# Three map steps and three convolution rounds to a tick, and spectral matmuls placed by tile shape, in a two-layer convolution kernel

## The chip, the cores and the metric

The kernel runs on one core of one Trainium2 chip. The metric is device microseconds of one launch. All arithmetic is float32. TensorE is called PE in the profile, its weight loads PEld, VectorE DVE, ScalarE ACT, GpSimd POOL and SyncE SP.

## The reference, cut to what matters

The input is `x`, 8 batch elements of 8 channels of 512 x 512. Two layers follow each other, each with a group normalization `_gn` (4 groups of two channels) in front and a residual around it:

```python
x = x + L0(_gn(x))      # spectral layer
x = x + L1(_gn(x))      # coupled map, hidden convolution, gates
```

L0 takes every second row and column, goes to the spectrum (`rfft2`), keeps 8 x 4 low modes, mixes the channels there with complex weights, and synthesizes the result back on all 512 x 512 points:

```python
out2 = einsum('bixy,ioxy->boxy', FW1[low modes], w)      # mode by mode
tmp  = einsum('boxw,xz->bozw', out2, E1)                 # over the rows
x2   = real(einsum('bozw,wi->bozi', tmp, E2)) / (Ws*Hs)  # over the columns
```

L1 has three parts: 15 steps of a coupled map, a hidden convolution (3x3 to 128 channels, ReLU, 1x1 back to 8, sigmoid), and a gate that blends both:

```python
for _ in range(15):
    mapped = 3.9 * grid * (1 - grid)
    physics = 0.7 * mapped + 0.3 * conv3x3_per_channel(mapped)
    grid = 0.85 * physics + 0.15 * drive
h   = relu(conv3x3(x, Wp, bp));  nca = sigmoid(conv1x1(h, Wu, bu))
g   = sigmoid(conv1x1(relu(conv3x3(concat(x, cml, nca), Wg1)), Wg2))
out = g * cml + (1 - g) * nca
```

## The kernel before, in words

The program is one straight list of instructions, recorded by Python loops; `keep_order` pins the order on every engine to that of the source. So the loops below decide what stands behind what on each engine's queue.

**Map steps.** `Slabs` holds one of 4 sets per half of the channels: 16 slabs of 32 rows each, with halos, as one tile `m`. A last set `Tail` closes the bottom rows. An element has 9 sets and each takes 15 steps, so 135 steps. `convolve` (L524) is 48 matmuls of 32x32 tiles into a half of PSUM, `settle` drains it (VectorE L537, ScalarE L543), adds to the drive on POOL at steps 1 and 13 (L516, L547), and `renew` exchanges the halo rows by four DMAs from POOL's queue (L570, L571). The list `slots` orders the steps: step 1 of every set of a phase, then step 2 of every set, and so on. The first phase of an element has 4 sets, the second 5. So a set comes back 4 or 5 slots later, and by then its halo must have landed. At step 15 a set leaves (`leave`, L596).

**Rounds.** `Hidden.round` (L723) is one of 128 rounds of the hidden convolution of an element: 12 matmuls of 32x128 tiles into a PSUM half; ScalarE (L729) drains one pair of banks to `h`, VectorE (L731) the other. `Hidden.point` (L742) is the 1x1 convolution of finished rounds in 128x32 tiles; four rounds are summed in `y`, on which ScalarE then runs the sigmoid (L755).

**Gates.** `Gate` covers 12 image rows, 43 to an element, one element behind the map: loads of `gin` and `mix`, `conv` (L793, 128x32 tiles; POOL L798, VectorE L799 and L803), `point` (L810; sigmoid L814, POOL L816) and `finish` (VectorE L821, store L828).

**Spectral work.** `layer0` is a generator for the element after the present one. Every `yield` ends a piece and says when the next may run. The pieces are: statistics and row transform of a channel (L329, L333: 128x128 tiles), averages over partitions (`group_stats`, L300 and L308: 128x128), the column transform (L358), the mode mix on VectorE, `over_rows` of a channel (L396: 16x32) and `synthesis` of half a channel (L428: two products of 8x128, then one add L431 and two statistics L433 on VectorE).

**The tick.** `work` records one tick: two map steps (`near` and `far` half of PSUM), `others.finish()`, loads (`transfers`), up to two rounds, and then, in the banks left, a gate's convolution, spectral pieces, the points, and the gate product of an earlier tick's gate. The outer loop runs 68 ticks per element and spreads 128 rounds over them:

```python
ticks = (second.end - at + 1) // 2
quota = [(t + 1) * (rounds - done) // ticks for t in range(ticks)]
```

The last element has 56 rounds beside its steps; its other 72 rounds and all its 43 gates run after the last step. Ahead of element 0's first steps stand its own spectral layer and 8 rounds. `Slots` hands out 20 tile buffers of 8 KB per partition between the sets and the others (`SHARED`, `MORE` and `LEAST` bound the share of the others), and `AHEAD` is how many slots ahead of a phase its loads (`dE`, `dO`) may begin.

Of the kernel before, what the change touches and what calls it, by code (L numbers as in the profile page):

```python
# [41 lines left out]
P = 128  # L42
# [12 lines left out]
LONG, LATER, NEXT = -1, -2, -3  # L55
GATES_FROM, SPECTRAL_FROM = 1, 2
# [9 lines left out]
SLOTS, SHARED, MORE, LEAST = 20, 5, 8, 3  # L66
AHEAD, PAUSE = 12, 6
# [50 lines left out]
def conv_layers(ctx: ExitStack, tc: tile.TileContext, a, out):  # L118
# [79 lines left out]
    avg = cp.tile([P, P], F32, name="avg")  # L198
# [14 lines left out]
    e1 = cp.tile([16, N], F32, name="e1")  # L213
    e2 = cp.tile([P, N], F32, name="e2")
    om = cp.tile([16, C + 3, 8], F32, name="om")
# [6 lines left out]
    def sines():  # L222
# [14 lines left out]
        nc.scalar.dma_start(out=e1[8:], in_=t)  # L237
# [58 lines left out]
    def group_stats(mv, n, bank):  # L296

        mean = sm.tile([P, n], F32, name=f"mean{n}")
        ps = bank[-1][:, 0]
        nc.tensor.matmul(ps[:, :n], avg, mv[:, :, 0], start=True, stop=True)  # L300
        nc.vector.tensor_copy(mean, ps[:, :n])
        var = sm.tile([P, n], F32, name=f"var{n}")
        nc.vector.tensor_tensor(var, mv[:, :, 0], mean, ALU.subtract)
        nc.vector.tensor_tensor(var, var, var, ALU.mult)
        nc.vector.tensor_tensor(var, var, mv[:, :, 1], ALU.add)
        yield LATER
        ps = bank[-1][:, 0]
        nc.tensor.matmul(ps[:, :n], avg, var, start=True, stop=True)  # L308
        std = sm.tile([P, n], F32, name=f"std{n}")
        nc.scalar.activation(std, ps[:, :n], AF.Sqrt, bias=eps)  # L310
        rstd = sm.tile([P, n], F32, name=f"rstd{n}")
        nc.vector.reciprocal(rstd, std)
        return mean, rstd, std

    def layer0(e, bank):


        def one():
            return bank[-1][:, 0]

        st = sm.tile([P, C, 4, 6], F32, name="st")
        mys = sm.tile([P, C, 2, 32], F32, name="mys")


        for c in range(C):
            yield c
# [3 lines left out]
            my = one()[:, :64].rearrange("p (h k) -> p h k", h=2)  # L330
            for h in range(2):
                for j in range(2):
                    nc.tensor.matmul(  # L333
                        my[:, h], xt[:, 2 * j, h * NS : (h + 1) * NS : 2], dft_y[:, j],
                        start=(j == 0), stop=(j == 1),
                    )
# [3 lines left out]
        yield NEXT  # L340
# [10 lines left out]
        wmix, ts = row([16, 2, C, C, 4], "wmix"), row([16, 2, C, C, 4], "ts")  # L351
        nc.sync.dma_start(out=wmix, in_=a["wmix"])
        yield LATER
        mx = one()[:, : C * 8].rearrange("p (c k) -> p c k", k=8)
# [8 lines left out]
        nc.vector.tensor_copy(f, mx[:16].rearrange("p c (q k) -> p c q k", q=2))  # L363

# [12 lines left out]
        yield LATER  # L377
        re = total(0, 0, 1, 1, ALU.subtract, "re")
        yield LATER
# [4 lines left out]
        back = sm.tile([16, C, 4], F32, name="back_re")  # L384
        nc.vector.tensor_scalar(back, re, on_sin, -1.0, ALU.mult, ALU.mult)
        nc.vector.tensor_scalar(re, re, on_cos, None, ALU.mult)
        nc.vector.scalar_tensor_tensor(om[:, :C, 0:4], im, on_sin, re, ALU.mult, ALU.add)
        nc.vector.scalar_tensor_tensor(om[:, :C, 4:8], im, on_cos, back, ALU.mult, ALU.add)
        yield LATER
# [3 lines left out]
        def over_rows(c):  # L393
            ps = one()
            for at in range(0, P, 32):
                nc.tensor.matmul(  # L396
                    ps[at : at + 32], om[:, c : c + 4].rearrange("p c k -> p (c k)"), e1, start=True, stop=True, tile_position=(0, at)
# [39 lines left out]
        for c in range(C):  # L437
            yield C + c
            ty, xt = ty_next, e.x[C + c]
            if c % 2 == 0:  # L440
                st = sm.tile([P, 2, 4, 6], F32, name="st1", bufs=2)
            synthesis(ty, xt, st[:, c % 2], 0)
            if closing:
                yield LATER
                next(closing)
                yield LATER
                next(closing, None)
                closing = None
            if c + 1 < C:
                yield  # L450
                ty_next = over_rows(c + 1)
            yield LONG
            synthesis(ty, xt, st[:, c % 2], 1)
            if c % 2:
                closing = close(c // 2, aggregate(st, 1))
        for kind in (NEXT, LATER):
            yield kind
            next(closing, None)
# [11 lines left out]
    class Slabs:  # L470
# [122 lines left out]
        def leave(self):  # L593
# [4 lines left out]
            def store():  # L598
# [6 lines left out]
                later(1, lambda: sets.drop(m))  # L605
# [50 lines left out]
    class Phase:  # L656
# [12 lines left out]
        def ready(self, k, o, n):  # L669

            s = self.sets[k]
            due = self.at + k <= n + 1
# [7 lines left out]
        def squares(self, n):  # L680
            while self.squared < len(self.sets) and sets.room():
                if not self.ready(self.squared, 0, n + 2):
# [12 lines left out]
    class Hidden:  # L695
# [19 lines left out]
        def round(self, ps, after, settled):  # L715
# [12 lines left out]
            h = wk.tile([P, 4, N], F32, tag="h", name="h", bufs=2)  # L728
# [9 lines left out]
        def point(self, ps):  # L738

            for r, h in self.hs:  # L740
                for g in range(4):
                    nc.tensor.matmul(  # L742
                        ps[32 * g : 32 * g + 32], w_u[:, r % 4], h[:, g],
                        start=(r == self.hs[0][0]), stop=(r == self.hs[-1][0]),
                        tile_position=(0, 32 * g),
                    )
            if self.hs[0][0] % 4 == 0:
                self.y = wk.tile([P, N], F32, tag="y", name="y", bufs=1)
# [3 lines left out]
            self.hs.clear()  # L752
# [84 lines left out]
    class Element:  # L837


        def __init__(self, b):  # L840
# [15 lines left out]
            self.bank = []  # L856
            self.pieces, self.need = layer0(self, self.bank), None

        def fetch(self):

            if self.fetched < 2 * C and shared.room() > 0 and len(self.x) < self.most():
# [4 lines left out]
        def most(self):  # L866
            return 2 if self.fetched < C else 4 if self.fetched < 2 * C else 0
# [9 lines left out]
        def spectral(self, ps, n, longs):  # L877

            need = self.need
            if need == NEXT and now[0] <= self.last:  # L880
                return False
            if not self.pieces or need == LATER and n or need is not None and need >= LONG and longs:
                return False
            if need is not None and need >= 0 and now[0] <= self.at.get(need, now[0]):
                return False
            self.bank.append(ps)
            self.need, self.last = next(self.pieces, self), now[0]
            self.bank.clear()
            if self.need is self:
                self.pieces, self.need = None, None  # L890
            return True

    class Others:


        def __init__(self):
            self.before, self.after, self.limit, self.lag = None, None, 2, 0
            self.mapped, self.paused, self.closed = deque(), False, False
            self.loaded, self.convolved, self.pointed = deque(), deque(), deque()
            self.longs = 0  # L900

        def feed(self, t):
# [3 lines left out]
            spectral = after and after.pieces  # L906
            spectral = spectral and (t >= SPECTRAL_FROM or not e)
            kept = max(0, after.most() - len(after.x)) if spectral else 0
            while e and e.gates and t >= GATES_FROM and not (self.paused or self.closed):
                if len(self.loaded) == self.limit or shared.room() - kept < 2:  # L910
# [6 lines left out]
            if spectral:  # L917
                after.fetch()
# [8 lines left out]
        def point(self, ps):  # L927
            if not (self.convolved and self.convolved[0].at < now[0]):
                return False
            g = self.convolved.popleft()  # L930
            g.point(ps)
            self.pointed.append(g)
            return True

        def spectral(self, banks):
            if not self.after:
                return
            for n, ps in enumerate(banks):
                long = self.after.need is not None and self.after.need >= LONG
                if not self.after.spectral(ps, n, self.longs):  # L940
                    return
                self.longs += long

        def gate(self, ps):
            self.longs = 0
            if not (self.loaded and self.loaded[0].at + self.lag < now[0]):
                return False
            g = self.loaded.popleft()
            g.conv(ps)
# [219 lines left out]
```

## Time and profile before

| | before |
|---|---|
| median of 3 runs | 9446.41 us |
| lowest and highest | 9430.03 and 9450.78 us |
| the profiled execution, its own time | 9442.09 us |
| its span | 9440.3 us |
| mean granted TensorE clock | 0.986 |
| busy PE, DVE, ACT, POOL | 9039.4, 5657.6, 4072.3, 3367.1 us |
| DMA | 1327.07 MB, mean 141 GB/s |

The span is what the hardware profiler saw from the first to the last instruction. A float32 product is two records in it, so the 48 matmuls of a step are 96. A matmul's end is modelled, so the distance from the start of one group to the start of the next tells more than the length of a group. In a list of groups, "idle" is the time in which the engine did nothing just before them, and behind it stands what ended most of it; "issue" means that the profile shows nothing that was waited for.

### The profile page before, as it was taken

The numbers are of one execution on the slowest core, as the hardware profiler recorded it, in microseconds if no ns is written. First come the engines' busy times: TensorE is split into PE (matmuls) and PEld (weight loads), VectorE is DVE, ScalarE is ACT, GpSimd is POOL, SyncE is SP. The second block draws the span as 40 slices with busy tenths as digits, with TensorE's granted clock in tenths as the row PEclk, the third lists the DMA queues.
The fourth block names the chain that finished last, engine by engine and source line by source line (L and its number), as shares of the span: only waits on it lengthen the run. The fifth ranks groups of instructions, "written<-read, shape, count | busy, mean of one in ns | idle before, by whom it ended". The sixth has DMA issues, their size and how long they took to land. (4 is left out here: it accounts for less than half of the span.)

```text
span 9440.3 us, 331607 instructions
## 1 busy us (share of the span) xinstructions
PE 9039.4 (96%) x148976; PEld 4068.9 (43%) x148976; DVE 5657.6 (60%) x5820; ACT 4072.3 (43%) x4285; POOL 3367.1 (36%) x4440
## 2 busy tenths in 40 slices
PE   6999999999999999999999999999999999999989
PEld 2444444444444444444444444444444444434433
DVE  5665566655666556665566555665566655555655
ACT  2444444444444444444444444444444444434422
POOL 3232333334333343433434333343433434343422
PEclk9999999999999999999999999999999999999999
DMA  4241365565645656655566556565565665565488
GB/s 148 87 128 35 90 168 136 146 142 136 164 129 150 143 127 160 157 138 139 145 149 165 137 125 156 129 169 139 127 169 136 165 138 117 141 155 124 109 198 207
DMA packets 697405, 1327.07 MB, mean 141 GB/s; under 512 B 146938, under 2 KB 152442, under 8 KB 668498
## 3 DMA queue, kind: packets, MB, share of 16 engines
q1 hardware_dynamic: 591840, 1244.38, 52.1%
q0 software_dynamic: 101792, 60.33, 3.1%
q8 instruction: 1171, 19.19, 0.9%
q14 instruction: 248, 2.03, 0.1%
q10 hardware_dynamic: 2354, 1.14, 0.0%
HBM read 977.48 MB, written 270.61 MB: 132 GB/s over the span
## 5 line engine op out<-in xcount | busy, mean ns | idle before, releaser
L524 PE MATMUL pair<-m,band 32*32 32x512 f32 x103680 | 3703.2, 604 | 159.3 <-issue 103.3
L543 ACT ACTIVATE m<-m 128x1024 f32<-128x1024 f32 x2016 | 2125.7, 1055 | 2458.2 <-DVE m L537 2396.4
L723 PE MATMUL pair<-cols,w_p 32*128 32x511 f32 (+1 forms) x24576 | 2863.4, 604 | 73.7 <-DMA cols<-xn 29.4
L524 PEld LDWEIGHTS pair<-m,band 32*32 32x32 f32 x103680 | 1997.7, 103 | 1788.1 <-issue 997.9
L570 POOL DMA_DIRECT2D m<-m x1568 | 861.4, 549 | 3927.7 <-ACT m L543 3851.5
L537 DVE SCALAR_TENSOR_TENSOR m<-pair,dO 128x1024 f32<-128x1024 f32 x1152 | 1357.0, 1220 | 1172.7 <-PE pair L524 1021.8
L723 PEld LDWEIGHTS pair<-cols,w_p 32*128 32x128 f32 x24576 | 1307.6, 187 | 1647.1 <-issue 1148.9
L731 DVE TENSOR_SCALAR h<-pair,b_p 128x1024 f32<-128x1024 f32 x1024 | 1312.8, 1283 | 905.5 <-PE pair L723 898.8
L537 DVE SCALAR_TENSOR_TENSOR m<-pair,dE 128x1024 f32<-128x1024 f32 x1008 | 1187.7, 1220 | 1064.3 <-PE pair L524 911.2
L729 ACT ACTIVATE h<-pair,b_p 128x1024 f32<-128x1024 f32 x1024 | 1140.0, 1114 | 923.3 <-PE pair L723 923.0
L742 PE MATMUL pair<-h,w_u 128*32 128x512 f32 x8192 | 1051.8, 606 | 39.3 <-ACT h L729 35.0
L793 PE MATMUL pair<-gin,w_g 128*32 128x511 f32 (+1 forms) x8256 | 962.2, 598 | 11.3 <-DMA gin<-nca 7.9
L816 POOL TENSOR_TENSOR mix<-mix 96x512 f32<-96x512 f32 x344 | 437.7, 1272 | 1278.7 <-ACT mix L814 1236.4
L571 POOL DMA_DIRECT2D m<-m x1568 | 841.3, 537 | 30.3 <-issue 27.2
L742 PEld LDWEIGHTS pair<-h,w_u 128*32 128x32 f32 x8192 | 244.7, 110 | 690.9 <-issue 347.8
L755 ACT ACTIVATE y<-y,b_u 128x512 f32<-128x512 f32 x256 | 184.8, 722 | 823.3 <-DVE y L751 823.3
L793 PEld LDWEIGHTS pair<-gin,w_g 128*32 128x32 f32 x8256 | 235.3, 110 | 686.8 <-issue 462.9
L798 POOL TENSOR_TENSOR mix<-mix 96x512 f32<-96x512 f32 x344 | 444.2, 1291 | 14.2 <-DMA mix<-nca 9.8
L547 POOL TENSOR_SCALAR dO<-dO 128x2048 f32<-128x2048 f32 x72 | 391.7, 5440 | 115.0 <-DVE m L537 114.0
L749 ACT COPY y<-pair 128x512 f32<-128x512 f32 x256 | 149.8, 585 | 624.2 <-PE pair L742 486.5
L516 POOL TENSOR_SCALAR dO<-dO,base 128x512 f32<-128x512 f32 x288 | 208.8, 735 | 574.6 <-DMA dO<-xn 532.7
L821 DVE SCALAR_TENSOR_TENSOR mix<-mix,back 96x512 f32<-96x512 f32 x344 | 329.1, 957 | 138.5 <-POOL mix L816 138.5
(90 smaller groups left out, 3337.1 us busy)
## 6 DMA issues: line engine op xcount, KB each, us to landing
gin<-xn SPq DMA_DIRECT2D x344, 384.0 KB
cols<-xn SPq DMA_DIRECT2D x256, 512.0 KB
x<-in_x SPq DMA_DIRECT2D x120, 1024.0 KB
gin<-cml SPq DMA_DIRECT2D x344, 320.0 KB
gin<-nca SPq DMA_DIRECT2D x344, 320.0 KB
dE<-xn SPq DMA_DIRECT2D x288, 256.0 KB
dO<-xn SPq DMA_DIRECT2D x288, 256.0 KB
mix<-xn SPq DMA_DIRECT2D x344, 192.0 KB
```

Source lines behind the costliest of these rows:

```text
L524: nc.tensor.matmul(ps[h // 2][32 * t : 32 * t + 32, h % 2], band[at, self.channel(step - 1, h, t), dx], m[at, t, dx : dx + N], start=(n == ...
L537: nc.vector.scalar_tensor_tensor(u[:, at], ps[q], FLOOR, d[:, at], ALU.max, ALU.add)
L543: nc.scalar.square(u[:, at], u[:, at])
L570: nc.gpsimd.dma_start(out=view(tb, rb, dims), in_=view(ta, ra, dims))
L571: nc.gpsimd.dma_start(out=view(ta, ra + s, dims), in_=view(tb, rb + s, dims))
L723: nc.tensor.matmul(ps[g // 2][:, g % 2, lo:hi], w_p[p, dx, i % 2], self.cols[p, i // 2, at : at + hi - lo], start=(n == 0), stop=(n == 2), ...
L729: nc.scalar.activation(h[:, :2], ps[0], AF.Relu, bias=b_p)
L731: nc.vector.tensor_scalar(h[:, 2:], ps[1], b_p, 0.0, ALU.add, ALU.max)
L742: nc.tensor.matmul(ps[32 * g : 32 * g + 32], w_u[:, r % 4], h[:, g], start=(r == self.hs[0][0]), stop=(r == self.hs[-1][0]), tile_position ...
L793: nc.tensor.matmul(ps[32 * j : 32 * j + 32, lo:hi], gband[:, dx], gin[:, j, at : at + hi - lo], start=(n == 0), stop=(n == 2), tile_positi ...
L798: nc.gpsimd.tensor_tensor(d, d, ng, ALU.subtract)
L816: nc.gpsimd.tensor_tensor(d, d, mix[: GR * C, 2], ALU.mult)
```

## The change

A tick has three map steps and up to three rounds instead of two and two. PSUM halves alternate from one use to the next (`half()`). Behind the rounds stand the pieces of kind `WIDE`: both halves of a channel's synthesis in one tick, in the other PSUM half. If one was placed, the 128x32 work of that tick uses the half of the last round. That work is: an `EARLY` spectral piece, a gate's convolution, the points (in one or two groups, as rounds of two sums can meet in a tick), a second gate or one or two `LATE` pieces, and the gate products of the same tick's gates; then gate loads. The row transform, the averages and `over_rows` become 128x32 tiles: four column tiles for the first two, and for the last `e1` and `om` are padded with zeros to 128 rows. `h` has three buffers and `y` two, the slots are 19, and up to two channels of `x` are loaded in a tick. After the last step every tick takes three rounds and up to two gates, of which the first waits three ticks.

```diff
-LONG, LATER, NEXT = -1, -2, -3
-GATES_FROM, SPECTRAL_FROM = 1, 2
+TICK = 3
+WIDE, EARLY, LATE = "wide", "early", "late"
+GATES_FROM, SPECTRAL_FROM = 1, 0
 SHIFTS = ((1, 0, N, 0), (0, 1, N, 0), (2, 0, N - 1, 1))
@@ -63,8 +64,8 @@
 TAIL_RENEW = 7
 TAIL_ROWS = ((1, SLAB - STEPS + TAIL_RENEW - 1), (STEPS - TAIL_RENEW + 1, SLAB))
 assert TAIL_AT + TAIL_ROWS[0][1] == N - SLAB + TAIL_ROWS[1][0]
-SLOTS, SHARED, MORE, LEAST = 20, 5, 8, 3
-AHEAD, PAUSE = 12, 6
+SLOTS, SHARED, MORE, LEAST = 19, 4, 7, 3
+AHEAD = 12
...
+    e1 = cp.tile([P, N], F32, name="e1")
+    nc.gpsimd.memset(e1, 0.0)
...
+        def averaged(v):
+            ps = bank[-1]
+            for at in range(0, P, 32):
+                nc.tensor.matmul(
+                    ps[at : at + 32, :n], avg, v, start=True, stop=True, tile_position=(0, at)
+                )
+            return ps[:, :n]
...
-            yield c
+            yield (LATE if c % 2 else EARLY), c
             xt = e.x[c]
             for j in range(4):
                 nc.vector.bn_stats(st[:, c, j], xt[:, j])
-            my = one()[:, :64].rearrange("p (h k) -> p h k", h=2)
+            my = bank[-1][:, :64].rearrange("p (h k) -> p h k", h=2)
             for h in range(2):
                 for j in range(2):
-                    nc.tensor.matmul(
-                        my[:, h], xt[:, 2 * j, h * NS : (h + 1) * NS : 2], dft_y[:, j],
-                        start=(j == 0), stop=(j == 1),
-                    )
+                    for q in range(4):
+                        at = h * NS + 64 * q
+                        nc.tensor.matmul(
+                            my[32 * q : 32 * q + 32, h], xt[:, 2 * j, at : at + 64 : 2],
+                            dft_y[:, j], start=(j == 0), stop=(j == 1),
+                            tile_position=(0, 32 * q),
+                        )
             nc.scalar.copy(mys[:, c], my)
             e.done_with(c)
...
-            yield C + c
-            ty, xt = ty_next, e.x[C + c]
+            yield WIDE, C + c
+            ty, xt, e.back_begun = ty_next, e.x[C + c], True
             if c % 2 == 0:
                 st = sm.tile([P, 2, 4, 6], F32, name="st1", bufs=2)
             synthesis(ty, xt, st[:, c % 2], 0)
+            yield WIDE, None
+            synthesis(ty, xt, st[:, c % 2], 1)
             if closing:
-                yield LATER
+                yield EARLY, None
                 next(closing)
-                yield LATER
+            if c + 1 < C:
+                yield LATE, None
+                ty_next = over_rows(c + 1)
+            if closing:
+                yield LATE, None
                 next(closing, None)
                 closing = None
-            if c + 1 < C:
-                yield
-                ty_next = over_rows(c + 1)
-            yield LONG
-            synthesis(ty, xt, st[:, c % 2], 1)
             if c % 2:
                 closing = close(c // 2, aggregate(st, 1))
-        for kind in (NEXT, LATER):
-            yield kind
+        for kind in (EARLY, LATE):
...
-            due = self.at + k <= n + 1
+            due = self.at + k < n + TICK
...
-            h = wk.tile([P, 4, N], F32, tag="h", name="h", bufs=2)
+            h = wk.tile([P, 4, N], F32, tag="h", name="h", bufs=TICK)
...
+        def sums(self):
+            groups = {}
             for r, h in self.hs:
+                groups.setdefault(r // 4, []).append((r, h))
+            self.hs.clear()
+            return list(groups.values())
+        def point(self, hs, ps):
+            for r, h in hs:
                 for g in range(4):
                     nc.tensor.matmul(
                         ps[32 * g : 32 * g + 32], w_u[:, r % 4], h[:, g],
-                        start=(r == self.hs[0][0]), stop=(r == self.hs[-1][0]),
+                        start=(r == hs[0][0]), stop=(r == hs[-1][0]),
                         tile_position=(0, 32 * g),
                     )
-            if self.hs[0][0] % 4 == 0:
-                self.y = wk.tile([P, N], F32, tag="y", name="y", bufs=1)
+            if hs[0][0] % 4 == 0:
+                self.y = wk.tile([P, N], F32, tag="y", name="y", bufs=2)
...
+            for _ in range(2):
+                if self.fetched == 2 * C or shared.room() == 0 or len(self.x) == self.most():
+                    break
                 self.x[self.fetched] = load_x(shared, self.b, self.fetched % C)
                 self.at[self.fetched] = now[0]
                 self.fetched += 1
-            return 2 if self.fetched < C else 4 if self.fetched < 2 * C else 0
+            if self.fetched == 2 * C:
+                return len(self.x)
+            return 4 if self.fetched < C or self.back_begun else 2
...
+        def conv(self, banks):
+            for n, ps in enumerate(banks):
+                if not self.loaded or now[0] < self.hold or self.loaded[0].at + self.lag > now[0]:
+                    return n
+                g = self.loaded.popleft()
+                g.conv(ps)
+                self.convolved.append((g, ps))
+            return len(banks)
+        def point(self):
+            while self.convolved:
+                g, ps = self.convolved.popleft()
+                g.point(ps)
+                self.pointed.append(g)
...
-    def work(steps, rounds, e, after, transfers, squares=lambda: None):
+    halves = pairs[:2], pairs[2:]
+    used = [0]
+    def work(steps, rounds, e, after, gates, transfers, squares=lambda: None):
+        def half():
+            used[0] += 1
+            return halves[used[0] % 2]
         settled = iter(())
-        near, far = pairs[:2], pairs[2:]
-        for (s, step), ps in zip(steps, (near, far)):
+        for n, (s, step) in enumerate(steps):
+            ps = half()
             s.convolve(step, ps)
             next(settled, None)
             settled = s.settle(step, ps)
             next(settled)
             others.finish()
+            if gates == 2:
+                others.load(1)
+                gates = 1
         others.finish()
         transfers()
-        for ps in (near, far)[:rounds]:
-            e.hidden.round(ps, after, settled)
+        for _ in range(rounds):
+            e.hidden.round(half(), after, settled)
         next(settled, None)
         squares()
-        if rounds == 2:
-            pairs.reverse()
-        elif rounds:
-            near, far = far, near
-        point = rounds and e.hidden.n % 2 == 0
-        gate = others.gate(near[0][:, 0])
-        others.spectral((far[0], far[1]) if gate else (near[0], far[0] if point else near[1]))
-        if point:
-            e.hidden.point(near[1][:, 0])
-        last = others.point((near[0] if point else near[1])[:, 1])
-        if not last:
-            others.spectral([near[0] if gate or point else near[1]])
-        if rounds == 0 and gate or rounds == 1 and not (gate or point or last or after):
-            pairs.reverse()
+        if not others.spectral(WIDE, halves[(used[0] + 1) % 2]):
+            used[0] += 1
+        b = [ps[:, i] for ps in halves[used[0] % 2] for i in range(2)]
+        others.spectral(EARLY, b[3:])
+        others.conv(b[:1])
+        groups = e.hidden.sums()
+        for hs, ps in zip(groups, b[1:3]):
+            e.hidden.point(hs, ps)
+        if not others.conv(b[3:]):
+            others.spectral(LATE, [b[1] if len(groups) == 2 else b[2], b[3]])
+        others.point()
+        others.load(gates)
...
-        steps = [slots[i] for i in (at, at + 1) if 0 <= i < len(slots)]
-        work(steps, rounds, e, after and after.hidden, transfers, squares)
-    for at in range(-FIRST_ROUNDS, 0, 2):
-        turn(at, 2, e, None, -1)
+        steps = [slots[i] for i in range(at, at + TICK) if 0 <= i < len(slots)]
+        work(steps, rounds, e, after and after.hidden, gates, transfers, squares)
...
+        open_ = [
+            t >= GATES_FROM and at + TICK * t < second.end - AHEAD
+            and not first.end - AHEAD + 3 <= at + TICK * t < first.end + 3
+            for t in range(ticks)
+        ]
...
+            left = len(others.before.gates) if others.before else 0
+            gates = open_[t] + (left > sum(open_[t:]) and not (after and after.pieces))
+            turn(at, min(more, TICK), e, after, gates)
+            at += TICK
...
+    others.after, others.hold, others.lag = None, now[0] + 3, 2
+    sets.most = shared.most = SLOTS
+    while e.hidden.n < ROUNDS or others.mapped or others.busy():
+        turn(at, min(TICK, ROUNDS - e.hidden.n), e, None, 2 if len(others.loaded) <= 4 else 0)
+        at += TICK
```

## The prediction

> **What bounds the kernel now.** I read the page's engine rows first, then TensorE's stretches in order of time, then TensorE's waits.
>
> ```profile
> PE 9039.4 (96%) x148976; PEld 4068.9 (43%) x148976; DVE 5657.6 (60%) x5820; ACT 4072.3 (43%) x4285; POOL 3367.1 (36%) x4440
> ```
>
> TensorE is busy 96% of the span, the next engine 60%. So the time is the sum of TensorE's stretches plus what stops it. In the view of one engine in order of time (start, length, engine, line, operation, tiles, tile shape, count), one whole tick of before is:
>
> ```profile
> 4189.91 6.58 PE L524 MATMUL pair<-m,band 32*32 32x512 f32 x192
> 4196.42 5.43 PE L723 MATMUL pair<-cols,w_p 32*128 32x512 f32 x48
> 4201.78 2.78 PE L793 MATMUL pair<-gin,w_g 128*32 128x512 f32 x24
> 4204.37 1.90 PE L742 MATMUL pair<-h,w_u 128*32 128x512 f32 x16
> 4206.09 1.03 PE L810 MATMUL pair<-mix,w_g 128*32 128x512 f32 x6
> 4207.05 6.58 PE L524 MATMUL pair<-m,band 32*32 32x512 f32 x192
> ```
>
> Start to start: two map steps 6.51 us, two rounds 5.36, gate and points 5.27. Nothing waits here. A "section" below is a run of matmuls of one tile shape. Its fixed price comes from sections of half or double content, in the same view:
>
> ```profile
> 4260.70 2.85 PE L723 MATMUL pair<-cols,w_p 32*128 32x512 f32 x24
> 4263.49 2.78 PE L793 MATMUL pair<-gin,w_g 128*32 128x512 f32 x24
> ...
> 8917.87 12.92 PE L524 MATMUL pair<-m,band 32*32 32x512 f32 x384
> 8930.72 2.85 PE L723 MATMUL pair<-cols,w_p 32*128 32x512 f32 x24
> ```
>
> One round takes 2.79 us, two 5.36: a round is 2.57 (six waves of 0.4285: the tiles of a wave stream their 512 columns side by side) and a section's fixed part 0.21. Four steps take 12.85, two 6.51: two steps are 6.34, fixed part 0.17. In the 128x32 sections the last two waves (L810) take 0.96 instead of 0.86: fixed part 0.11. Ticks with spectral work look like this:
>
> ```profile
> 4007.27 1.02 PE L428 MATMUL pair<-e,ty 8*128 8x512 f32 x4
> 4008.22 1.92 PE L742 MATMUL pair<-h,w_u 128*32 128x512 f32 x16
> 4010.21 0.38 PE L300 MATMUL pair<-mv,avg 128*128 128x1 f32 x2
> ...
> 4039.60 1.07 PE L742 MATMUL pair<-h,w_u 128*32 128x512 f32 x8
> 4040.88 1.23 PE L742 MATMUL pair<-h,w_u 128*32 128x512 f32 x8 [0.21 <-ACT h L729]
> ```
>
> Half a synthesis costs a whole pair of waves (0.95 us). The second pair shows points with no gate ahead of them: 4039.60 to the next step at 4042.04 is 2.44 us for 1.83 of work, because the last round's h is still on ScalarE. What stops TensorE most:
>
> ```profile
> PE pair L524 <- issue: 103.3, 69, 3.9
> PE pair L742 <- ACT h L729: 35.0, 93, 6.9
> PE pair L723 <- DMA cols<-xn: 29.4, 3, 14.3
> ...
> PE pair L524 <- DMA m<-m: 22.7, 13, 4.2
> PE pair L723 <- DVE m L537: 19.6, 8, 3.2
> ```
>
> The largest wait has no releaser (69 times, 1.5 us each, in map steps).
>
> [...] queue q8 moved 1171 packets, 19.19 MB, thus 16 KB per 254 of the 297952 weight loads and matmuls, and the stops without releaser each end shortly after such a packet. [...] the mean granted clock is 0.986, so about 0.014 x 9440 = 132 us are lost to half clock, mostly beside stops.
>
> **The change, part by part.** From the order of both built programs I count sections: 2025 before, 1160 after. At undisturbed lengths the 2025 sum to 8700 us: steps 3515, rounds and synthesis 2869, 128x32 work 2147, other shapes 170. The remaining 740 us of the 9440 are start-up (about 115), half clock and stops.
>
> *Ticks of three.* Step sections 537 to 360: 177 x 0.17 = 30 us. Sections with rounds 565 to 387: 178 x 0.21 = 38. Sections of 128x32 work 664 to 397: 267 x 0.11 to 0.14 = 32. All on TensorE, so all on the path. Steps, rounds, gates, halo DMAs and their bytes are as many as before, so their queues carry the same totals.
>
> *Synthesis as one wave.* 128 half-syntheses of two products, each two waves or 0.86 us, become 64 whole ones with all four row tiles in the same two waves (a round already runs four row tiles at once): 55 us. Own sections of synthesis alone go from 59 to 8: 8 us.
>
> *The rest as 128x32.* The 16x32 product (L396, 0.99 us to the next stretch at its median) becomes a 128-row one: two waves, 0.86, 64 times: 8 us. The averages (0.31) become four column tiles and the row transform (1.06 per channel) 32 small matmuls. No row has them in this form. The nearest is L358, 64 matmuls with weights in 1.68 us, 26 ns each, thus 0.21 and 0.85 us. If 32-column weight loads (110 ns each at L742) do not overlap, they cost 0.9 and 3.5 us, together up to 220 us more. Against that: L742's four loads start within 21 ns of each other. I take 0.25 and 0.9: a gain of 15 us, plus or minus 10. Below that, nothing.
>
> The sum is 30 + 38 + 32 + 63 + 8 + 15 = 186 us less work in the sections.
>
> *Waits that go.* In a tick with three rounds two points (1.7 us) precede the third, and h of the last round (ScalarE 1.11, VectorE 1.28 us) is ready. Sections that hold points ran 113 us over their undisturbed length in all (196 of them, points alone, had a median of 0.59). Some 25 ticks of two rounds without a gate keep 0.45 each: 100 us gone. The waits between single spectral products (L396, L428, L308: about 35 us, with half clock 55) go too.
>
> *Waits that come.* In the 64 ticks with synthesis the 128x32 section uses the PSUM half of the last round: it waits for VectorE's 1.28 us less the wave, 0.4 us. Then VectorE has two adds and four statistics (2 x 1.21 + 4 x 0.69 = 5.2 us) ahead of the gate's L803, so the gate's point product at the end of the section waits another 0.7 to 1.3 (0.7 with the points between, which I take; 1.3 where an average and its small VectorE steps come first). 1.1 x 64 = 70 us, and 20 of half clock. Ticks with two gates wait 0.3 us, 30 times: 10. The queues: POOL gets halo issues of three steps per tick instead of two. In the traced tick a step's four issues end 5.9 to 7.2 us after its matmuls and a landing takes some 5 us, so 13. Two of three steps come due a tick later, 24 us; before it was two ticks less one step, 31. That covers it, also with POOL's 5.4 us L547. In the last element (one round a tick, 17 us instead of 21) L547 no longer fits: about 20 stops of 2 us, 40. SP runs past the same loads, in lumps half as large again (two x tiles at once, gate loads after the points); y has two buffers, so its store no longer holds ScalarE. One slot less for tiles costs me nothing, as 15 tiles of a phase still fit in 15 or 16; without that cover dE or dO comes a tick late, some 10 us per phase. I leave the stops without releaser as they are: three steps need 576 instructions in a row, but loads now start before the rounds, where instructions are used slowly.
>
> Start-up and tail: 15 us less. The DMA share is 0.90 in the tail, so that it gives little:
>
> ```profile
> 9090.00:9190.00 100.00, 100.00 (x878) 35.76 (x870) 58.75 (x53) 31.63 (x37) 29.71 (x26) 1.00 0.90 213
> ```
>
> Total: -186 - 100 - 55 - 15 + 70 + 20 + 10 + 40 = -216. The profiled execution took 9442.1 (span 9440.3), so it would take 9226; it lies 4 under the median of 9446.4, and in terms of the median that is 9230 us.
>
> **Rivals.** *VectorE and the halo take half* (chance 0.23): waits in synthesis ticks of 3 us (POOL's L547 in the same tick blocking L821) and stops in every late phase: 100 to 150 us more, 9350. For it: VectorE is at 60% and its work is bunched; against: L821 waited for POOL only 138.5 us in all. *Instruction lines* (0.11, slower): [...] Its place is the second and third step of a tick, its price 1.5 us a stop (103.3 / 69) plus clock. It decides from about 150 stops more than the 69, when the 216 us are gone; at 190 more, 9500. Against: the loads would have to delay a refill in half of all ticks. *Balance* (0.05): half the stops and half the waits, within 0.2%, 9446. That the change does not do what it says is excluded by the order of the program: one section a shape and tick.
>
> **How the numbers follow.** My forecast, 9230 (0.61), spans 9110 (stops without releaser fall with the ticks by a third, and synthesis ticks wait for nothing) to 9300. With the rivals the range is 9090 to 9420. A difference under 0.2%, 19 us, a measurement of this kernel cannot tell from none. Faster 0.61 + 0.23 = 0.84, same 0.05, slower 0.11.
>
> **What would show it.** Right: 360 step sections of 9.68 us, rounds of three in 7.92, an eight-matmul synthesis wave of 0.86 behind them, no wait of the points for h. Wrong: more than 150 waits of map steps without releaser; waits for the halo exchange above 100 us; row-transform stretches above 1.5 us a channel; the 128x32 sections of synthesis ticks more than 3 us over their work.

## The result, and the profile after

The changed kernel takes 9975.52 us (median of 4 runs, 9965.90 to 9985.13); the kernel before takes 9440.95 us in the 4 runs made beside it. The ratio is 1.0567, with a 95% interval of 1.0548 to 1.0585: **slower by 5.7%**, where 2.3% faster was forecast and the range ended at 9420. The profiled execution has a span of 9964.1 us, 524 more than before's 9440.3, and a mean granted clock of 0.976 (before 0.986).

The engine row of the page of the changed kernel (busy time, share of the span, instructions):

```profile
PE 8922.2 (90%) x150992; PEld 4159.7 (42%) x150992; DVE 5677.5 (57%) x5844; ACT 4095.4 (41%) x4283; POOL 3371.7 (34%) x4441
```

TensorE has less to do than before (8922 us instead of 9039), as forecast, but is busy for only 90% of the span instead of 96%. So this is not a matter of more work; TensorE now stops. TensorE's waits (what waits, for whom, us in total, times, longest) say for whom:

```profile
PE pair L760 <- DVE mix L820: 462.0, 291, 4.8
PE pair L534 <- issue: 93.5, 68, 3.8
PE pair L827 <- DVE y L769: 57.4, 71, 0.8
...
PE pair L827 <- ACT y L767: 44.7, 57, 4.1
...
PE pair L534 <- DMA m<-m: 5.4, 2, 4.3
```

The first line was not there before: the points (L760) wait 291 times for VectorE's L820, the bias and ReLU of the gate. L820 reads the sums that the gate's convolution (L810) has just made. The stops without releaser (L534, issue) are as many as before, and waits for the halo (m<-m) have all but gone. TensorE in order of time shows one whole tick (start, length, engine, line, operation, tiles, tile shape, count, and idle time before it with its releaser):

```profile
4101.15 9.75 PE L534 MATMUL pair<-m,band 32*32 32x512 f32 x288
4110.83 6.27 PE L733 MATMUL pair<-cols,w_p 32*128 32x512 f32 x52
4117.34 2.84 PE L733 MATMUL pair<-cols,w_p 32*128 32x512 f32 x20 [0.24 <-DVE h L741]
4120.11 2.78 PE L810 MATMUL pair<-gin,w_g 128*32 128x512 f32 x24
4123.84 2.78 PE L760 MATMUL pair<-h,w_u 128*32 128x512 f32 x24 [0.94 <-DVE mix L820]
4126.44 1.03 PE L827 MATMUL pair<-mix,w_g 128*32 128x512 f32 x6
4127.40 2.98 PE L534 MATMUL pair<-m,band 32*32 32x512 f32 x82
```

Three steps take 9.68 us start to start, as worked out. The gate's matmuls begin at 4120.11 and the points at 4123.84, 3.73 us later. Six waves with nothing between them are 2.57. All engines in order of time, in another tick without spectral work:

```profile
3351.68 2.78 PE L810 MATMUL pair<-gin,w_g 128*32 128x512 f32 x24
...
3354.60 0.75 DVE L820 TENSOR_SCALAR mix<-pair,b_g 128x512 f32<-128x512 f32 x1 [0.81 <-PE pair L810]
...
3355.41 2.78 PE L760 MATMUL pair<-h,w_u 128*32 128x512 f32 x24 [0.95 <-DVE mix L820]
```

L820 starts 0.14 us after the gate's last matmul ends, runs 0.75 us, and the points start 0.06 us after it. In a tick with a synthesis VectorE gets to L820 much later. The same view:

```profile
1442.71 2.78 PE L810 MATMUL pair<-gin,w_g 128*32 128x512 f32 x24 [0.40 <-ACT h L739]
1442.74 1.21 DVE L440 TENSOR_TENSOR x<-x,pair 128x1024 f32<-128x1024 f32 x1
1443.99 1.29 DVE L442 BATCH_NORM_STATS2 st<-x 128x6 f32<-128x512 f32 x2
1445.19 1.20 DVE L440 TENSOR_TENSOR x<-x,pair 128x1024 f32<-128x1024 f32 x1
1446.43 1.29 DVE L442 BATCH_NORM_STATS2 st<-x 128x6 f32<-128x512 f32 x2
1447.64 0.73 DVE L816 SCALAR_TENSOR_TENSOR mix<-mix,back 96x512 f32<-96x512 f32 x1
1448.29 0.74 DVE L820 TENSOR_SCALAR mix<-pair,b_g 128x512 f32<-128x512 f32 x1
1449.08 5.35 PE L760 MATMUL pair<-h,w_u 128*32 128x512 f32 x24 [3.59 <-DVE mix L820]
```

The adds and statistics of the synthesis are ahead of L816 and L820 in VectorE's queue. The points wait 3.59 us for them, and then run for 5.35 us instead of 2.78: the stop cost the clock as well. The trace has TensorE at half clock (granted 0.50) from 1448.26 to 1455.09.

Sorted by section (start to start less the length that a section has where nothing disturbs it, all summed), the span comes apart like this:

| us | before | after | difference |
|---|---|---|---|
| undisturbed length, 2025 and 1160 sections | 8700 | 8523 | -177 |
| over it: sections of map steps | 295 | 215 | -80 |
| over it: sections of rounds | 187 | 189 | +2 |
| over it: sections of 128x32 work | 126 | 998 | +872 |
| over it: other shapes (nearly all are 128x32 after) | 93 | -7 | -100 |

The sum is 517 of the 524 us. Of the 998 us, 353 lie in the 64 sections behind a synthesis (5.5 us each), 604 in 338 others, and 41 in the first section of the program, whose start-up stood under other shapes before. Lost half clock, an estimate from the two mean clocks, is inside these figures: 0.014 x 9440 = 132 us before, 0.024 x 9964 = 239 after.

**Why points wait for a bank that they don't write.** With `b = [ps[:, i] for ps in halves[used[0] % 2] for i in range(2)]` the four banks are dealt as both banks of one pair tile, then both of the other. The gate's convolution takes `b[0]`, the first points take `b[1]`: another bank, but of the same tile. Before, gate and points had different tiles (`near[0]`, `near[1]`). The wait stands in the program: in the trace, the first point at each of the 291 places carries a wait on the semaphore that VectorE's instructions count up, and the point starts when L820 has ended (0.05 us later at the median). Whether the chip would hold the points up without that semaphore, no run here shows. That the wait is there because of the tile is what the experiments test, by moving the banks. (A tile for each bank alone, which would be the most direct test, was not run.)

### The profile page after: what moved, and what is told of

It reads as the page before. It is cut to its first block, busy times and chain, and to the rows that moved or that the text cites. A ratio compares the mean times of both kernels' runs of the same rounds, so it can differ in the third digit from the quotient of the medians.

```text
span 9964.1 us, 334600 instructions
## 1 busy us (share of the span) xinstructions
PE 8922.2 (90%) x150992; PEld 4159.7 (42%) x150992; DVE 5677.5 (57%) x5844; ACT 4095.4 (41%) x4283; POOL 3371.7 (34%) x4441
## 5 line engine op out<-in xcount | busy, mean ns | idle before, releaser
L534 PE MATMUL pair<-m,band 32*32 32x512 f32 x103680 | 3620.0, 604 | 108.8 <-issue 93.5
L733 PE MATMUL pair<-cols,w_p 32*128 32x511 f32 (+1 forms) x24576 | 2798.3, 596 | 59.3 <-DMA cols<-xn 32.7
L534 PEld LDWEIGHTS pair<-m,band 32*32 32x32 f32 x103680 | 2172.9, 103 | 1514.3 <-issue 822.7
L547 DVE SCALAR_TENSOR_TENSOR m<-pair,dO 128x1024 f32<-128x1024 f32 x1152 | 1355.7, 1219 | 1117.6 <-PE pair L534 951.7
L547 DVE SCALAR_TENSOR_TENSOR m<-pair,dE 128x1024 f32<-128x1024 f32 x1008 | 1187.2, 1219 | 998.7 <-PE pair L534 786.5
L739 ACT ACTIVATE h<-pair,b_p 128x1024 f32<-128x1024 f32 x1024 | 1141.1, 1114 | 1186.7 <-PE pair L733 1185.2
L760 PE MATMUL pair<-h,w_u 128*32 128x512 f32 x8192 | 1065.8, 648 | 475.2 <-DVE mix L820 462.0
L810 PE MATMUL pair<-gin,w_g 128*32 128x511 f32 (+1 forms) x8256 | 980.1, 609 | 63.4 <-ACT y L767 23.5
L760 PEld LDWEIGHTS pair<-h,w_u 128*32 128x32 f32 x8192 | 249.6, 115 | 1240.6 <-DVE mix L820 670.4
L810 PEld LDWEIGHTS pair<-gin,w_g 128*32 128x32 f32 x8256 | 245.1, 111 | 709.6 <-issue 581.3
L827 PE MATMUL pair<-mix,w_g 128*32 128x512 f32 x2064 | 366.3, 608 | 161.9 <-DVE y L769 57.4
L769 DVE TENSOR_TENSOR y<-y,pair 128x512 f32<-128x512 f32 x280 | 192.1, 686 | 495.7 <-PE pair L760 489.5
L831 ACT ACTIVATE mix<-pair,b_g 96x512 f32<-96x512 f32 x344 | 235.2, 684 | 509.0 <-PE pair L827 374.0
L820 DVE TENSOR_SCALAR mix<-pair,b_g 128x512 f32<-128x512 f32 x344 | 257.1, 747 | 309.9 <-PE pair L810 309.9
```

The costliest lines, as they stand in the source:

```text
L534: nc.tensor.matmul(ps[h // 2][32 * t : 32 * t + 32, h % 2], band[at, self.channel(step - 1, h, t), dx], m[at, t, dx : dx + N], start=(n == ...
L547: nc.vector.scalar_tensor_tensor(u[:, at], ps[q], FLOOR, d[:, at], ALU.max, ALU.add)
L733: nc.tensor.matmul(ps[g // 2][:, g % 2, lo:hi], w_p[p, dx, i % 2], self.cols[p, i // 2, at : at + hi - lo], start=(n == 0), stop=(n == 2), ...
L739: nc.scalar.activation(h[:, :2], ps[0], AF.Relu, bias=b_p)
L760: nc.tensor.matmul(ps[32 * g : 32 * g + 32], w_u[:, r % 4], h[:, g], start=(r == hs[0][0]), stop=(r == hs[-1][0]), tile_position=(0, 32 * g),)
L810: nc.tensor.matmul(ps[32 * j : 32 * j + 32, lo:hi], gband[:, dx], gin[:, j, at : at + hi - lo], start=(n == 0), stop=(n == 2), tile_positi ...
```

## The experiments

Theory A: the points wait because they share a pair tile with the gate; other banks take the 462 us away. Theory B: VectorE is behind with its work in the longer ticks, whatever the banks are. Theory C: longer bursts of steps run out of fetched instructions.

**Banks, first try.** In the changed kernel, gate and first points get different tiles, but the second group of points shares the tile of the first:

```diff
-        b = [ps[:, i] for ps in halves[used[0] % 2] for i in range(2)]
+        here = halves[used[0] % 2]
+        b = [here[p][:, i] for p, i in ((0, 0), (1, 0), (1, 1), (0, 1))]
```

> The changed kernel with the four banks of the 128x32 work dealt otherwise: the gate's convolution in the first pair, both groups of points in the second pair, second gate or late spectral pieces in the first pair. Theory A (the points wait because they write the same PSUM pair as the gate's convolution, whose other bank VectorE still has to read at L820): waits of the points for L820 fall from 462 us to under 40, and the time from 9975 us to 9450 to 9580, since two groups of points now share a pair and the second waits for y up to 0.9 us in about half of the ticks. Rival B (VectorE is late in long ticks, whatever the bank): the points wait as long for another VectorE operation, and the time stays above 9850. Rival C (the refill of TensorE's instructions in three steps): waits without releaser are the loss, and the time stays within 1%.

Measured: 9860.84 us, 1.0436 (1.0421 to 1.0452). The gain is only 115 us, so A's expectation missed. The time lies above 9850, where B put it. TensorE's largest wait in this kernel:

```profile
PE pair L760 <- DVE y L769: 184.6, 149, 4.2
```

The wait of L760 for L820 is gone, but one of the same kind has come: now the second points wait for VectorE's read (L769) of the first points' bank, in the other half of the same tile. This fits A, with the wait only moved, and it fits B, which expected the points to wait for another operation of VectorE. The next run separates them.

**Banks, second try.** The gate has one tile, the first points the other, and the second points are back in the gate's. Against the first try:

```diff
-        b = [here[p][:, i] for p, i in ((0, 0), (1, 0), (1, 1), (0, 1))]
+        b = [here[p][:, i] for p, i in ((0, 0), (1, 0), (0, 1), (1, 1))]
```

> As the last, but the second group of points goes into the gate's pair and the late pieces into the second pair, so that the two groups do not share a pair. Theory A: waits of the points for L820 under 60 us, some waits of the gate product for y, time 9400 to 9520, the best of these. Rival B: above 9850. Rival C: within 1% of 9975.

Measured: 9507.76 us, 1.0061 (1.0046 to 1.0076): 468 us less than the changed kernel, by one line that alters no work. TensorE in order of time:

```profile
4014.86 2.78 PE L810 MATMUL pair<-gin,w_g 128*32 128x512 f32 x24
4017.46 2.76 PE L760 MATMUL pair<-h,w_u 128*32 128x512 f32 x24
4020.03 1.03 PE L827 MATMUL pair<-mix,w_g 128*32 128x512 f32 x6
```

From gate to points it is now 2.60 us instead of 3.73. The waits:

```profile
PE pair L534 <- issue: 120.5, 79, 4.0
PE pair L827 <- ACT y L767: 58.2, 67, 1.2
PE pair L760 <- DVE mix L820: 54.3, 43, 2.7
...
PE pair L760 <- DVE mean L309: 50.4, 23, 4.7
```

291 waits on L820 have become 43, and the clock is back at 0.984. Theory A holds for 468 us. This deal has not parted every pair of neighbours, though. Of the 43 waits left none is of the first points: all are of later ones, and the second group lies in the gate's tile. The 23 waits for L309 are of first points: L309 reads an average from the fourth bank, which is in their tile. And the gate's product goes into the gate's own bank, behind the second points in the same tile (L827 for L767). What is left above before, 0.6% where the sections' sum should have made it faster, is so at least in part the same fault.

**The same fault put into the kernel before.** If A is right, before becomes slower by it:

```diff
-            e.hidden.point(near[1][:, 0])
-        last = others.point((near[0] if point else near[1])[:, 1])
+            e.hidden.point(near[0][:, 1] if gate else near[1][:, 0])
+        last = others.point((near[0] if point and not gate else near[1])[:, 1])
```

> The kernel before, with one thing made as in the changed one: where a tick has a gate's convolution, the points go into the other bank of the same PSUM pair, and the gate product into the other pair. Theory A: the points wait for VectorE's L803 in some 250 ticks, at least 1.1 us each, in all 300 to 450 us, and the time rises from 9441 to 9750 to 9950 us. Rivals B and C: nothing in the length of the tick changes, so 9441 plus or minus 30.

Measured: 9702.68 us, 1.0272 (1.0255 to 1.0289), 252 us more. It is smaller than expected, but the sign and the place are right. The waits, and one tick:

```profile
PE pair L742 <- DVE mix L803: 208.5, 212, 4.2
```

```profile
4198.87 2.78 PE L793 MATMUL pair<-gin,w_g 128*32 128x512 f32 x24
4202.59 1.92 PE L742 MATMUL pair<-h,w_u 128*32 128x512 f32 x16 [0.94 <-DVE mix L803]
```

The wait is 0.94 us, as in the changed kernel, although this kernel has ticks of two and the old synthesis. So neither ticks of three nor the new synthesis is needed for it.

**Ticks of two in the changed kernel** (`TICK = 2`, banks as changed; `h` then has two buffers, as their number is `TICK`). B and C expect a gain, A as many waits for L820 and some 100 us for more changes of tile shape.

> The changed kernel with TICK = 2, all else kept: tile placement, synthesis wave, 128x32 products, shared pair. Theory A: as many gates share a pair with points, so the waits for L820 stay at 400 to 500 us, and the step sections become 540 again [...]: 9950 to 10150. Rival B (long ticks): waits for L820 fall by half, 9700 or less. Rival C: 384 instead of 576 instructions in a row, waits of steps without releaser fall clearly below the 93 us, time below 9800.

Measured: 10301.11 us, 1.0899 (1.0879 to 1.0918). The waits:

```profile
PE pair L760 <- DVE mix L820: 493.2, 310, 4.8
...
PE pair L760 <- ACT h L739: 94.0, 200, 5.1
PE pair L534 <- issue: 82.6, 59, 4.1
```

Shorter bursts have 11 us less of stops without releaser and lose far more elsewhere, so C is out. B as a cause by itself is out as well: shorter ticks wait no less for L820, and in the second try VectorE has the same work in the same order. The size was above what A expected. In part this is the points waiting again for h of the last round (L739, 200 times, 84 us more than in the changed kernel), as in the kernel before.

**Ticks of two with the banks mended** (the second try, with `TICK = 2`), to price the ticks alone:

> The kernel of e2_gate_alone_first with TICK = 2. What ticks of three are worth by themselves: 180 sections fewer of each of the three shapes, by the prediction about 100 us, so 9590 to 9640. If two steps in a row are kinder to TensorE's instruction refill or to VectorE (rivals B and C), 9510 or less.

Measured: 9880.07 us, 1.0465 (1.0444 to 1.0486), 372 us above the second try. The expectation, which counted the tile changes, missed by some 250. The undisturbed sections sum to 8604 us instead of 8523 (1694 of them): these 81 us are the changes. The rest is stops:

```profile
PE pair L534 <- issue: 148.1, 93, 3.8
PE pair L760 <- ACT h L739: 89.1, 196, 4.6
PE pair L404 <- DVE mix L820: 57.7, 28, 2.7
```

So in this program ticks of three are worth much more than their tile changes. One reason is that the third round covers the time in which h is made: the points' wait for L739 is 8.0 us in the second try and 89.1 here. The other 210 us are spread over many waits and the clock (0.981 instead of 0.984), and were not taken apart.

**Old tile shapes** (the second try with the averages, the row transform and the product at L404 as before: 128x128 and 16 rows):

```diff
-            for at in range(0, P, 32):
-                nc.tensor.matmul(
-                    ps[at : at + 32, :n], avg, v, start=True, stop=True, tile_position=(0, at)
-                )
+            nc.tensor.matmul(ps[:, :n], avg, v, start=True, stop=True)
...
-                    for q in range(4):
...
+                    nc.tensor.matmul(
+                        my[:, h], xt[:, 2 * j, h * NS : (h + 1) * NS : 2], dft_y[:, j],
+                        start=(j == 0), stop=(j == 1),
+                    )
```

> The kernel of e2_gate_alone_first with the tile shapes of before for the row transform and averages (128x128) and the product over rows (16 rows, 32 columns), at the same places. By the prediction's working the 128x32 forms save 23 us [...]: 9540 to 9570. If the many small column-tile matmuls cost as much as they save: 9500 plus or minus 15.

Measured: 9565.51 us, 1.0133 (1.0116 to 1.0149), 58 us above the second try. So this part of the change is a gain, of the size that was expected.

**What the second try still waits for.** In its 64 sections behind a synthesis there are still 218 us over the undisturbed length (353 before the mend). Two remedies, each on top of the second try. Half a synthesis at a time, so that VectorE gets one add and two statistics in a lump:

```diff
-        if not others.spectral(WIDE, halves[(used[0] + 1) % 2]):
+        if not others.spectral(WIDE, halves[(used[0] + 1) % 2][:1]):
```

> The kernel of e2_gate_alone_first (9508 us) with half a channel's synthesis to a tick instead of both halves. VectorE then has 2.6 instead of 5.2 us ahead of the gate's L820. If what is left of the loss is VectorE's bunched work in the 64 synthesis ticks (their 128x32 sections run about 170 us over their work in e2), most of that goes and 64 x 0.86 = 55 us of waves come back: 9410 to 9470. If it is not, 9550 to 9580.

Measured: 9437.03 us, 0.9997 (0.9986 to 1.0009), 71 us below the second try: no difference from before is left. The lump is a cost, although twice as many synthesis sections are paid for, an estimated 64 x 0.86 = 55 us of waves.

The other: the gate's ReLU goes to ScalarE, which has no synthesis work ahead of it.

```diff
-            nc.vector.tensor_scalar(self.mix[:, 3], ps, b_g1, 0.0, ALU.add, ALU.max)
+            nc.scalar.activation(self.mix[:, 3], ps, AF.Relu, bias=b_g1)
```

> The kernel of e2_gate_alone_first with the gate's ReLU (L820) on ScalarE instead of VectorE, so that it no longer stands behind the synthesis on VectorE's queue. Theory A with bunching: waits for the gate's ReLU fall from about 107 us (L760, L827 and L404 together) to under 40, time 9380 to 9440. If the shared pair was all: 9500 plus or minus 20.

Measured: 9449.80 us, 1.0007 (1.0000 to 1.0014), 58 us below the second try and just short of the expectation. Both together:

> e5_half_synthesis and e6_relu_on_scalar together: the gate alone first, half a synthesis to a tick, the gate's ReLU on ScalarE. Each alone took 71 and 58 us off the 9508 of e2. If they take away different waits of VectorE's queue: 9380 to 9420, faster than before by 0.3 to 0.7%. If they take away the same ones: 9430 to 9445.

Measured: 9398.51 us, 0.9966 (0.9952 to 0.9979), 109 us below the second try; the two alone sum to 129. But the kernel before took 9432.64 us beside this run and 9450.62 beside the second try. By the ratios the gain is 90 us, and 60 and 51 for the two alone. Either way they take mostly different waits away. In this kernel the waits start with

```profile
PE pair L534 <- issue: 105.7, 76, 4.8
PE pair L760 <- DVE mean L309: 37.2, 23, 2.3
PE pair L827 <- ACT y L767: 36.8, 49, 1.2
```

The last of these is the gate's point product (L827), which follows two groups of points and waits for ScalarE's read of one. Last experiment, on top of both: in such ticks the product goes to the free bank.

```diff
-        if not others.conv(b[3:]):
-            others.spectral(LATE, [b[1] if len(groups) == 2 else b[2], b[3]])
-        others.point()
+        taken = others.conv(b[3:])
+        if not taken:
+            taken = others.spectral(LATE, [b[1] if len(groups) == 2 else b[2], b[3]])
+        others.point(b[3] if len(groups) == 2 and not taken else None)
...
```

> e9_half_and_relu, and in ticks with two groups of points and nothing in the fourth bank the gate's product goes into that bank, in the other pair, so that it does not wait for y's read of the second group (about 60 us of L827 waiting for L767 or L769 in e6). Theory A: 30 to 60 us below e9_half_and_relu. If the pair doesn't matter there: within 10 us of it.

Measured: 9386.71 us, 0.9946 (0.9929 to 0.9963). The wait has fallen from 36.8 to 10.3 us (24 times), and the list now begins:

```profile
PE pair L534 <- issue: 114.9, 79, 3.7
PE pair L810 <- DMA gin<-nca: 43.1, 15, 6.7
PE pair L760 <- DVE mean L309: 37.3, 23, 2.3
```

The median fell by only 12 us, where A expected 30 to 60, and the intervals overlap, so this step's own worth stays open. The version as a whole is faster than before by 0.5% and has the lowest median of all. Its clock is 0.986, before's own. The 37.3 us of L309 are the shared tile of the second try, which nothing here has parted.

## Why the prediction was wrong, point by point

**Work in the sections: right.** -186 was forecast, and -177 came out at undisturbed lengths, with 1160 sections. Three steps take 9.680 us (forecast 9.68) and three rounds 7.928 (7.92). The row transform came out better: 0.39 us a channel (taken: 0.9), its 2048 matmuls busy for 31.8 us against 78.3 before. The fear that 32-column weight loads would not overlap did not come true: 32 of them one after another, at 110 ns, would be 3.5 us.

**Waits that go: right in place.** Waits of the points for h fell from 35.0 to 10.0 us, and the single products' wait for it (L396, 15.8 us before) is gone. TensorE did not keep the time, since the points in the same place met the new wait.

**Waits that come: the step that failed.** It said of the 64 synthesis ticks that VectorE's 5.2 us hold up "the gate's point product at the end of the section", and gave 1.1 x 64 = 70 us and 20 for clock. The 5.2 us were right, but who stood behind them was wrong: the points wait as well, ahead of the product and with nothing to cover it. These sections cost 353 us instead of 90. In the ordinary ticks the working charged nothing for a gate followed by points, and 0.3 us x 30 where there are two gates. Measured were 604 us in 338 sections, some 50 of them stops of averages that were sections of their own before (93 less the start-up's 41). The 48 sections with two gates ran 2.4 us over at their median. The error behind both: banks were taken as independent, where the wait follows the tile that holds two of them. The order of both programs was read for sections, not for which tile each bank of `b` belongs to. The line that builds `b`, read beside `near[0]` and `near[1]` in the lines that it replaces, shows the shared tile.

**Halo and queues: too dear.** 40 us were charged for late exchanges, but the waits for m fell from 22.7 to 5.4 us. The sections of map steps lost 80 us of stops, some of it from here.

**Clock: mis-sized with the waits.** 20 us were charged, and about 107 more were lost (239 less 132), most of it behind the new stops, as at 1449.08: the trace has 99 stretches of half clock instead of 61.

**Rivals.** The slower side was held for *Instruction lines*, whose further stops did not come: 93.5 us in 68 stops against 103.3 in 69, with 576 instructions in a row. The trace of before shows 1171 packets of 16 KB on q8, a queue of the kind "instruction", and the stops of map steps without releaser end 1.2 to 1.7 us behind one of them. That 576 instructions in a row bring more such stops was the author's assumption; no run shows it. *VectorE and the halo* had the right engine and the right ticks (3 us a synthesis tick, measured 5.5), but another reason for the wait (POOL's L547), and stops for the halo, which did not come. It ended at 9350 because it too left out the ordinary gate ticks. The sign that the text gave for being wrong, 128x32 sections of synthesis ticks more than 3 us over their work, is what the trace shows: a median of 5.8.

**What remains open.** The forecast of 9230 would still not have been met with the banks right: the second try is at 9508. Of this distance the lump on VectorE and the ReLU behind it are 90 to 109 us, by experiment. The best version stands at 8523 plus some 55 of extra half waves in its sections and 9391 in its span, so that about 800 us of start-up, clock and stops are left, more than the 740 before. By section it has 319 us over the undisturbed length in 128x32 work, 258 in steps and 251 in rounds. In the rounds' share a part is the gate's convolution waiting for the half of the last round (L810 for L739: 22.1 us, 54 times). Why the stops in steps do not fall with the number of ticks was not tried.

## What to carry to other kernels

When banks are dealt anew, write down for each neighbouring pair of operations which *tile* each one has, not only which bank: a write into one bank of a two-bank tile here waits for the read of the other bank. Then walk the reading engine's queue up to that read, because everything in it is added to the wait (3.59 us behind a synthesis, 0.94 without one). A saving that is sure in the sections (177 us) is small beside a wait that comes back in most ticks (0.94 us and more, 291 times).

## What the runs showed of the hardware that was not expected

A stop of a few microseconds can cost most of its length once more in clock: after 3.59 us idle the next 24 matmuls took 5.35 us instead of 2.78, at a granted clock of 0.50. Of the 99 stretches of half clock in the changed kernel's trace, 95 last 3.41 or 6.83 us. Short stops hardly ever cost clock: after 0.94 us, at 4123.84, the length stayed at 2.78. Counted over this trace, a stretch of half clock begins in or within 3.5 us behind 97 of the 140 stops of TensorE of 2 us or more, and 3 of the 594 shorter ones.

Small matmuls with 32-column weights, placed in four column tiles, are cheap: the 32 records of a channel's row transform, with their loads, took 0.39 us at the median, 12 ns each, half of what the prediction's nearest case (L358, 26 ns) had.
